# When batch 1's query, scores and soft maximum are placed in the second Y phase

## Chip, cores and metric

The kernel runs on one core of a Trainium2 chip. The metric is the device time of one execution in microseconds. Before the change three runs took 453.0, 452.93 and 451.36 us (median 452.93); one more execution was profiled, and it took 451.54 us.

## What is computed

The input x has 2 batches of 1024 rows of 1024 values. Every row is normalised, and two matrices are applied to it. The first is a weight in which blocks of 32 x 32 are switched off by a mask; the second is a dense weight plus a sum of eight low-rank experts, mixed with coefficients that depend on the mean row of the batch.

```python
xn = layernorm(x)                                  # rows of 1024
w  = weight * block_mask                           # 32 x 32 blocks
s  = xn @ w.T + bias
q      = xn.mean(axis=1) @ Wq.T                    # one query per batch
coeffs = softmax(q @ lora_keys.T / sqrt(128))      # 8 experts
h      = einsum('bsi,eir->bser', xn, lora_down)    # rank 64 each
delta  = einsum('be,bser,ero->bso', coeffs, h, lora_up)
y      = xn @ W_org.T + delta
out    = x + s * silu(y)
```

The coefficients are one row of 8 numbers for each batch, and they need all 1024 normalised rows of that batch.

## The kernel before

The kernel folds the experts into the dense weight: for each batch it forms W_org + sum of coeff * down * up once, as tiles of 128 x 512, and then multiplies x with it. A fold needs the eight coefficients, so the chain from the row sums to the coefficients stands ahead of the first fold of a batch.

All large products are in float32 split in two parts: a value's high part (a rounded copy made by ScalarE) and the low rest (a subtraction on VectorE). A product takes three matmuls for each 128 of the inner dimension: high x high, high x low, low x high (lines 450, 453, 454 for the rows of batch 0). A tile of 128 rows by 512 columns is thus 24 matmuls.

The work is a long list in program order. First come the masked weight and the tiles of s for batch 0's first 512 columns, then two phases called "y" for batch 0, with eight tiles each (tile 0 to 7). Between the tiles of a phase, jobs for later stages are put in. In the second Y phase they are given by `jobs_c(i)`, called behind tile i: `s_mul` and `s_lo` prepare the other half of the masked weight (`s1`), one of eight inner tiles at a time (line 297 loads `ws`, 299 masks it on VectorE, 302 copies the high part on ScalarE, 307 takes the low part on VectorE); `wide_load`, `wide_a` and `wide_b` load and normalise the columns of batch 1 (lines 962, 963), with the row sums `xsum` as a by-product, and form sums of them (968).

Behind the second Y phase follow the tiles of s for batch 0's second half, with 16 folds for batch 1 between them (4, 4, 3, 3 and 2 behind the first five s tiles). A fold is 12 matmuls (414 to 416) on `dhi`, `dlo` (the `down` weights, 405 and 406) and `cut` (the `up` weights scaled by the coefficients, 392 on ScalarE and 393 on VectorE, made by `scale_up`). The last part, some 220 us, is batch 1 itself, in seven products for each two-by-two block of tiles (line 1211).

The coefficients of batch 1 come in four steps, a tuple that `coeffs(1)` returns:

- `steps[0]`, the row transposes: eight small transposes on TensorE (322) spread `xsum` over all partitions into two PSUM tiles, `xrow`
- `steps[1]`, the query: two products with accumulation on VectorE (346), `xrow` by `Wq`, and a join (350) that writes `qb`
- `steps[2]`, the scores: one matmul of `qb` with the keys (357, two passes in the records), three small VectorE instructions (359, 361, 362) and a power on GpSimd (364)
- `steps[3]`, the soft maximum: a sum, a reciprocal and two scalings on VectorE (370, 372, 377)

A step can also be put inside a tile: `split_at[(0, 1, i)]` names a step that goes between the first and the last 12 matmuls of tile i.

TensorE, VectorE, ScalarE and GpSimd run their instructions in the written order. The order of SyncE's queue, which issues most of the loads (SP), is made by a scheduler from that list. The evacuation of a tile (475 on ScalarE in a Y phase, 466 and 499 for a final s tile) is kept pending and written ahead of the next tile. `scale_up` takes one staging buffer from `misc` (`up_homes`) and three from a ring of six tiles, which `ws`, `us`, the `down` tile and the `W_org` tile of a fold share.

Of the kernel before, what the change touches and what calls it, by code (L numbers as in the profile page):

```python
# [32 lines left out]
def kernel(  # L33
# [492 lines left out]
    split_at = {}  # L526
# [6 lines left out]
    def phase(kind, b, h, w, final, jobs):  # L533

        for i in range(TPB):
            flush()
            if (b, h, i) in split_at:
                ps, part = open_gemm(b, i, w)
                part(0, 4)
                split_at[(b, h, i)]()  # L540
                part(4, NKT)
            else:
                ps = gemm(b, i, w)
            if final:
                pending.append(J(final_evac, kind, b, h, i, ps))
            else:
                pending.append(J(tile_evac, kind, b, h, i, ps))
            for job in jobs(i):
                job()
# [100 lines left out]
    with tc.manual_schedule(engines={mybir.EngineType.PE, mybir.EngineType.DVE, mybir.EngineType.Activation, mybir.EngineType.Pool}):  # L650
# [344 lines left out]
        steps = coeffs(1)  # L995

        def jobs_c(i):
            if i < 2:
                yield J(store_out, 1 - i)
            if i == 5:  # L1000
                yield steps[0]
                yield steps[1]
            if i == 6:
                yield steps[3]
                yield J(scale_up, 1, 0, up_homes)
            if i < 6:
                yield J(s_mul, s1, 1, i)
                yield J(s_lo, s1, 1, i)
            if i == 5:
                for kt in (6, 7):  # L1010
                    yield J(s_mul, s1, 1, kt)
                    yield J(s_lo, s1, 1, kt)
            if i in (0, 2):
                yield J(wide_load, 2 + i // 2, 0)
                yield J(wide_load, 2 + i // 2, 1)
            if i < 5:
                yield J((wide_b, wide_a)[i % 2], 1 + (i + 1) // 2)

        up_homes = [misc[:, 0, :]]
        split_at[(0, 1, 6)] = steps[2]  # L1020
        phase("y", 0, 1, y01, False, jobs_c)


# [341 lines left out]
```

## Time and profile before

| | |
|---|---|
| the three runs | 453.0, 452.93, 451.36 us |
| profiled execution, whole | 451.54 us |
| its span, first to last instruction | 449.8 us |
| mean granted TensorE clock | 0.998 |
| data moved, mean | 90.58 MB, 201 GB/s |
| second Y phase, tiles 6 and 7, with steps 0 to 2 | 189.4 to 203.7 us of the span |
| first s tile of the second half | 203.7 to 209.1 us |
| first fold of batch 1 | from 209.1 us |

The profile lists instructions with their start from the span's beginning and their duration, by engine: PE is TensorE's matmul, DVE VectorE, ACT ScalarE, POOL GpSimd. An idle time ahead of an instruction is shown with what ended it. Matmuls overlap: one of 512 columns has a modelled length of 0.39 us, but the next starts 0.227 us after it. What counts is therefore the distance from start to start.

### The profile page before, as it was taken

To read this page: it belongs to the slowest core of one execution; us is meant where nothing else is said; L and a number is where in the kernel's file an instruction comes from. 1 tells how busy PE (TensorE), PEld (TensorE's weight loads), DVE (VectorE), ACT (ScalarE), POOL (GpSimd) and SP (SyncE) were. 2 spreads that over 40 slices of the span, in tenths; PEclk is the share of its full clock that TensorE was granted. 3 is DMA by queue.
4 is the path that set the end of the run, shared out by engine and by line. 5 is a ranking of instruction groups with operands and counts; after the bars stand their busy time and mean duration, and the time that the engine had idled before them with its cause. 6 is when DMAs were issued, how large, how long until landed. Compare 5 with 4: busy or idle time off the path is not lost.

```text
span 449.8 us, 5786 instructions
## 1 busy us (share of the span) xinstructions
PE 439.7 (98%) x2058; PEld 363.3 (81%) x2058; DVE 289.4 (64%) x478; ACT 175.6 (39%) x291; POOL 76.6 (17%) x93
## 2 busy tenths in 40 slices
PE   7999999999999999999999999999999999999996
PEld 5789888888888888778888788888888888888885
DVE  5989777766528758876456667487556294365615
ACT  3676626454631221225233134067344322441520
POOL 3784210002220402221000000110020030002000
PEclk9999999999999999999999999999999999999999
DMA  8995406687796887797979797966183146218103
GB/s 272 390 345 207 143 25 206 215 265 217 250 306 179 267 248 251 268 346 259 286 219 311 218 306 197 302 176 189 40 180 127 66 110 172 93 24 209 49 1 117
DMA packets 47741, 90.58 MB, mean 201 GB/s; under 512 B 4816, under 2 KB 15328, under 8 KB 47712
## 3 DMA queue, kind: packets, MB, share of 16 engines
q1 hardware_dynamic: 30624, 66.08, 43.1%
q0 software_dynamic: 6624, 16.26, 15.7%
q10 hardware_dynamic: 10464, 7.87, 5.4%
q8 instruction: 16, 0.26, 0.3%
q14 instruction: 13, 0.11, 0.1%
HBM read 70.26 MB, written 19.93 MB: 201 GB/s over the span
## 4 chain that ended last, share of the span: by engine, by line
PE 73%; issue 10%; DMA 8%; DVE 4%; POOL 3%; SPq 0%; ACT 0%; POOLq 0%; DVEq 0%; ACTq 0%
PE acc_ps L1211 25%; PE py L1211 10%; PE acc_ps L450 8%; PE acc_ps L454 8%; PE acc_ps L453 8%; PE psw L416 5%; PE psw L415 5%; PE psw L414 5%; DMA ramp<-in_wT_dram 2%; DMA keys_sb<-in_keysT_dram 2%; POOL xv L524 2%; DMA ramp<-in_mask_dram 2%; DMA misc<-in_up_dram 1%; DMA xv<-xt 1%; POOL stash L502 1%
## 5 line engine op out<-in xcount | busy, mean ns | idle before, releaser
L1211 PE MATMUL acc_ps<-xw,ow 128*128 128x512 f32 (+1 forms) x492 | 113.2, 386 | 0.0
L1211 PEld LDWEIGHTS acc_ps<-xw,ow 128*128 128x128 f32 x492 | 91.0, 188 | 19.5
L450 PE MATMUL acc_ps<-slot,xgrp 128*128 128x512 f32 (+1 forms) x288 | 106.6, 370 | 0.1
L454 PE MATMUL acc_ps<-slot,xgrp 128*128 128x512 f32 (+1 forms) x288 | 105.7, 367 | 0.7 <-DVE xgrp L603 0.7
L453 PE MATMUL acc_ps<-slot,xgrp 128*128 128x512 f32 (+1 forms) x288 | 105.7, 367 | 0.6 <-DVE slot L591 0.2
L453 PEld LDWEIGHTS acc_ps<-slot,xgrp 128*128 128x128 f32 x288 | 54.3, 189 | 10.8 <-DVE slot L591 2.1
L454 PEld LDWEIGHTS acc_ps<-slot,xgrp 128*128 128x128 f32 x288 | 54.2, 188 | 10.2 <-DVE xgrp L603 1.1
L450 PEld LDWEIGHTS acc_ps<-slot,xgrp 128*128 128x128 f32 x288 | 54.3, 189 | 9.1 <-DVE stash L466 0.3
L416 PE MATMUL psw<-cut,dlo 128*128 128x512 f32 x128 | 50.1, 391 | 0.3 <-DVE dlo L406 0.3
L414 PE MATMUL psw<-cut,dhi 128*128 128x512 f32 x128 | 49.9, 390 | 0.0
L415 PE MATMUL psw<-cut,dhi 128*128 128x512 f32 x128 | 49.8, 389 | 0.0
L1211 PE MATMUL py<-xw,ow 128*128 128x512 f32 x192 | 46.9, 392 | 0.0
L1211 PEld LDWEIGHTS py<-xw,ow 128*128 128x128 f32 x192 | 36.1, 188 | 7.9
L1104 DVE TENSOR_TENSOR ow<-raw,ow 128x1024 fp32r<-128x1024 f32 (+1 forms) x32 | 34.5, 1088 | 9.9 <-ACT ow L1103 9.9
L405 ACT CAST dhi<-ds 128x512 fp32r<-128x512 f32 x32 | 19.7, 616 | 40.8 <-DMA ds<-in_down_dram 25.2
L502 POOL DMA_DIRECT2D stash<-in_x_dram x16 | 14.4, 899 | 117.6 <-DVE stash L499 117.6
L421 DVE TENSOR_TENSOR wo<-wo,psw 128x512 f32<-128x512 f32 x32 | 21.9, 685 | 13.2 <-PE psw L416 13.0
L406 DVE TENSOR_TENSOR dlo<-ds,dhi 128x512 fp32r<-128x512 f32 x32 | 22.0, 687 | 12.6 <-ACT dhi L405 12.5
L1103 ACT CAST ow<-raw 128x1024 fp32r<-128x1024 f32 (+1 forms) x32 | 29.4, 941 | 1.8 <-DVE wo L421 1.6
L416 PEld LDWEIGHTS psw<-cut,dlo 128*128 128x128 f32 x128 | 24.0, 188 | 5.8 <-DVE dlo L406 0.9
L415 PEld LDWEIGHTS psw<-cut,dhi 128*128 128x128 f32 x128 | 24.1, 188 | 5.1
L414 PEld LDWEIGHTS psw<-cut,dhi 128*128 128x128 f32 x128 | 24.0, 188 | 4.9
(180 smaller groups left out, 468.9 us busy)
## 6 DMA issues: line engine op xcount, KB each, us to landing
ds<-in_down_dram SPq DMA_DIRECT2D x32, 256.0 KB, 3.7
wo<-in_worgT_dram SPq DMA_DIRECT2D x32, 256.0 KB, 3.7
raw<-in_x_dram SPq DMA_DIRECT2D x11, 512.0 KB, 4.9
stash<-in_x_dram POOLq DMA_DIRECT2D x16, 256.0 KB, 4.8
raw<-in_wu_dram SPq DMA_DIRECT2D x8, 512.0 KB, 4.9
yu<-wo ACTq DMA_DIRECT2D x16, 256.0 KB, 4.5
raw<-yu SPq DMA_DIRECT2D x8, 512.0 KB, 3.7
out_dram<-stash ACTq DMA_DIRECT2D x14, 256.0 KB, 4.1
```

The lines of the kernel that those rows point to most:

```text
L405: nc.scalar.copy(dhi, ds)
L406: nc.vector.tensor_tensor(dlo, ds, dhi.bitcast(F32), ALU.subtract)
L414: nc.tensor.matmul(ps, lhsT=dhi[:, c, :], rhs=u[c][:, 0, :], start=c == 0, stop=False)
L415: nc.tensor.matmul(ps, lhsT=dhi[:, c, :], rhs=u[c][:, 1, :], start=False, stop=False)
L416: nc.tensor.matmul(ps, lhsT=dlo[:, c, :], rhs=u[c][:, 0, :], start=False, stop=c == 3)
L421: nc.vector.tensor_tensor(ws, ws, ps, ALU.add)
L450: nc.tensor.matmul(ps, lhsT=xs[:, kt, 0, cols], rhs=w[:, kt, 0, wc], start=kt == 0, stop=False)
L453: nc.tensor.matmul(ps, lhsT=xs[:, kt, 0, cols], rhs=w[:, kt, 1, wc], start=False, stop=False)
L454: nc.tensor.matmul(ps, lhsT=xs[:, kt, 1, cols], rhs=w[:, kt, 0, wc], start=False, stop=kt == NKT - 1)
L1103: nc.scalar.copy(o[:, a:b, 0], raw[:, a:b])
L1104: nc.vector.tensor_tensor(o[:, a:b, 1], raw[:, a:b], o[:, a:b, 0].bitcast(F32), ALU.subtract)
L1211: nc.tensor.matmul(ps, lhsT=o[:, a, wl, j, :], rhs=xw[j][:, m, xl, cols], start=start and j == 0 and k == 0, stop=j == 3 and k == 2, skip_ ...
```

## The change

Three of the four steps for batch 1's coefficients are placed later in the second Y phase, and the last moves with them.

```diff
         def jobs_c(i):
             if i < 2:
                 yield J(store_out, 1 - i)
-            if i == 5:
-                yield steps[0]
+            if i == 6:
                 yield steps[1]
-            if i == 6:
+            if i == 7:
                 yield steps[3]
                 yield J(scale_up, 1, 0, up_homes)
             if i < 6:
                 yield J(s_mul, s1, 1, i)
                 yield J(s_lo, s1, 1, i)
             if i == 5:
                 for kt in (6, 7):
                     yield J(s_mul, s1, 1, kt)
                     yield J(s_lo, s1, 1, kt)
...
         up_homes = [misc[:, 0, :]]
-        split_at[(0, 1, 6)] = steps[2]
+        split_at[(0, 1, 6)] = steps[0]
+        split_at[(0, 1, 7)] = steps[2]
         phase("y", 0, 1, y01, False, jobs_c)
```

| step | before | after |
|---|---|---|
| row transposes | behind tile 5 | in the middle of tile 6 |
| query | behind tile 5, ahead of the last three weight tiles of `s1` | behind tile 6, and so behind those three weight tiles |
| scores | in the middle of tile 6 | in the middle of tile 7 |
| soft maximum, first `scale_up` | behind tile 6 | behind tile 7 |

On ScalarE the evacuation of tile 6 comes ahead of the four scalings instead of behind them. On SyncE two loads of `misc` for batch 1 come behind the third `up` load and the first fold's two loads instead of ahead of them. GpSimd's order is the same.

## The prediction

> **What bounds the kernel now.** I read the page first, then the waits of TensorE (PE), then the timelines of PE, VectorE (DVE) and the DMA issues around the place of the change, and last the granted clock. The page says who sets the end:
>
> ```profile
> PE 439.7 (98%) x2058; PEld 363.3 (81%) x2058; DVE 289.4 (64%) x478; ACT 175.6 (39%) x291; POOL 76.6 (17%) x93
> ```
>
> PE is busy 439.7 of 449.8 us; ten microseconds are all that it idles. So a change of order is worth what it adds to or takes from PE's idle time. The waits view, for PE, gives the idle time by what ended it:
>
> ```profile
> PE sp L357 <- DVE qb L350: 1.1, 1, 1.1
> PE xrow L322 <- DVE bd L963: 0.7, 1, 0.7
> ...
> PE psw L416 <- DVE dlo L406: 0.3, 1, 0.3
> ```
>
> The first two belong to the edited lines: the scores matmul waits 1.1 us for the query, and the row transposes wait 0.7 us for the last row sum. The third line is the only one that the same view lists for 203 us to the end. From there on nothing can absorb a delay of PE, so a shift goes to the end of the kernel one for one. The timeline of PE shows the two places:
>
> ```profile
> 189.41 0.93 PE L322 MATMUL xrow<-ident,xsum 128*128 128x128 f32 x7
> 191.00 0.32 PE L322 MATMUL xrow<-ident,xsum 128*128 128x128 f32 x1 [0.67 <-DVE bd L963]
> 191.08 0.48 PE L450 MATMUL acc_ps<-slot,xgrp 128*128 128x512 f32 x1
> ...
> 195.18 0.36 PE L357 MATMUL sp<-keys_sb,qb 128*128 128x8 f32 x2 [1.08 <-DVE qb L350]
> 195.39 0.48 PE L450 MATMUL acc_ps<-slot,xgrp 128*128 128x512 f32 x1
> ```
>
> And the timeline of DVE shows what feeds them, and what stands behind the query today:
>
> ```profile
> 192.80 0.69 DVE L968 TENSOR_TENSOR xt<-bd,tt 128x512 f32<-128x512 f32 x1
> 193.40 0.68 DVE L346 SCALAR_TENSOR_TENSOR junk<-xrow,misc 128x512 f32<-128x512 f32 x1
> ...
> 194.74 0.29 DVE L350 TENSOR_TENSOR qb<-qh 128x128 f32<-128x128 f32 x1
> 195.26 0.69 DVE L299 TENSOR_TENSOR ws<-ws,m_sb 128x512 f32<-128x512 f32 x1 [0.23 <-DMA ws<-in_wT_dram]
> 196.64 0.69 DVE L307 TENSOR_TENSOR slot<-ws,slot 128x512 fp32r<-128x512 f32 x1 [0.69 <-ACT slot L302]
> ...
> 200.60 0.69 DVE L307 TENSOR_TENSOR slot<-ws,slot 128x512 fp32r<-128x512 f32 x1 [0.69 <-ACT slot L302]
> 201.21 0.16 DVE L359 TENSOR_SCALAR sc<-sp 128x8 f32<-128x8 f32 x1
> ```
>
> The reader is to see that three weight tiles (L299, then L302 on ScalarE, then L307) hold DVE from 195.26 to 201.21, two microseconds each, and that the first of them starts when its data lands, not when DVE is free. The tile view of these loads has the same: issued from 190.1 on, landed 5.1 us later at the earliest.
>
> ```profile
> L297 SPq DMA_DIRECT2D ws<-in_wT_dram x3: 371/372/423, 190.1 to 191.1; - x3
> ...
> DMA to landing us min/median/max: 5.1/5.8/6.0
> ```
>
> Last, the windows view of PE at the end of the span, where PE has nothing to do after about 446.06 (the columns are the stretch, its length, PE busy, and then the clock):
>
> ```profile
> 447.00:448.00 1.00, 0.00 (x0) 1.00 0.09 29
> ...
> 448.30:448.50 0.20, 0.00 (x0) 0.68 0.14 41
> 448.50:449.80 1.30, 0.00 (x0) 0.50 0.00 0
> ```
>
> The granted clock falls to half at about 448.37 (0.68 over 0.2 us means 0.07 us at full), some 2.3 us after the last matmul. The longest idle time before that, 1.59 us near the start, brought no drop.
>
> [...] the scores of batch 1 leave PE at about 195.5, yet L359 reads them at 201.21, behind the three weight tiles. [...]
>
> **The change part by part.** Nothing is added or removed: 8 transposes, 2 query products, one join, one score matmul, the soft maximum and four scalings are the same instructions. On PE the transposes go behind 12 more matmuls (half of tile 6), the score matmul behind 24 more (half of tile 7). On DVE, the two L346 and L350 change places with the six instructions of the weight tiles. ACT gets tile 6's evacuation ahead of the four scalings instead of behind; POOL keeps its order.
>
> *Row transposes.* Tile 5's last matmul starts at 189.18; the next may start at 189.41. Half a tile is 12 x 0.227 = 2.7 us, so the transposes come at 192.1. Their last input is there at 190.95. The 0.67 us of waiting is gone. Eight transposes at the spacing of the row of seven (0.66 us for six steps, 0.11 each) end at 193.0.
>
> *Query.* DVE is free at 193.4 as before, but its next instruction is now the first L299, whose data lands at about 195.2. The load is issued behind two others on SP, which wait for DVE work before the edit (L962, done at 189.7), so the landing stays. The three tiles then run to 201.21 as now. The query takes 194.74 - 193.40 = 1.34 us to the start of L350, which is thus 202.55; today the score matmul follows 0.44 us after that start, so it starts at 203.0.
>
> *Scores.* PE: second half of tile 6 from 193.0 to 195.75, first half of tile 7 to 198.5. Then it stands until 203.0: a wait of 4.5 us on L357, instead of 1.08. Behind it on PE are the other 12 matmuls of tile 7, the whole of the first s tile and the folds, which everybody waits for.
>
> *Sum on PE.* After 203.0: 0.2 for the scores, then 36 matmuls (half of tile 7, s tile 0) at 0.227 = 8.2, so the first fold at 211.4; the page's trace has it at 209.13. That is +2.3 us. (By waits: 4.5 new, against 0.67 and about 1.3 with its restart removed, and about 0.2 less for rounded spacing.)
>
> *Soft maximum and scaling behind it.* Today L359 at 201.21 leads to L377 at 204.01, the first L392 at 204.51 and the first fold's dlo (L406) at 208.19 to 208.88: 7.7 us. Now L359 starts at about 203.5, so dlo is done by 211.2. It is needed by the fold's third matmul, 211.4 + 0.45. It just fits, and the tile-6 evacuation (0.58 us on ACT), no longer between the scalings and dhi, adds to the slack. Cost nothing; if the cover goes, up to 1 us. The up loads and the first down and worg loads wait on buffers that the weight tiles free at unchanged times; the two misc<-xv loads go behind them on SP and behind L346, about 8 us later, and are first used at 213.2. Nothing.
>
> *The clock.* A wait of 4.5 us is [...] longer than the 2.3 us that sufficed at the end. If the clock halves during the wait, matmuls after 203.0 run at half rate [...]. [...] a gain is excluded, as 1.00 is what is granted now. I take 1.5: about 3 us of matmuls at half rate.
>
> Total +2.3 + 1.5 = +3.8 us. The profiled execution took 451.54 us (span 449.8 and 1.7 around it): 455.3. Its three neighbours are 451.36, 452.93 and 453.0, so this is one of the two quick ones; on the mean of the four, 452.2, I get 456.0, and 456.7 on the median 452.93. I take 456.0.
>
> **The rivals.**
> *No clock drop.* The wait is as worked out, but the clock stays at 1.00. [...] Against: half clock after 2.3 us at the end. 452.2 + 2.3 = 454.5.
>
> *The scaling becomes late too.* The chain from L359 to the fold's operands has 0.6 us of slack by my sum; if the loads of up or down land later by more, the first fold waits as well. Another 1 to 2 us: 457.5. Against: a clock drop gives the chain more slack.
>
> *The other side: the waits go and none comes.* The removed 0.67 and 1.1 to 1.3 us stay saved, 450.3 us. This happens if L350 is done when PE comes to the scores at 198.5, that is, starts by 198.06. The weight tiles take 5.95 us and the query 1.34, so the first L299 would have to start at 190.8. Its data lands 4.4 us after that and DVE is busy with L968 until 193.4. It needs the query to be ahead of the weight tiles on DVE; the program order puts it behind.
>
> **How the numbers follow.** Forecast (wait and clock drop) 0.70, no drop 0.16, late scaling 0.08, other side 0.06. About 0.5% (2.26 us) is what a measurement of this kernel can tell from no change. The forecast is slower by more than that in nine of ten cases, with the spread of the four times; the no-drop case, at +2.3, in half; the late scaling always. Slower 0.70 x 0.9 + 0.08 + 0.08 = 0.79, rounded to 0.78. The other side saves at most 2.0 us, just under the bound; faster 0.04, and the same 0.18. The range runs from 453.4, low in the no-drop case, to 458.4[...].
>
> **What would show it.** Right: in PE's waits, L322 gone, L357 on L350 with 4 to 4.7 us; on DVE, L346 at about 201.2 behind the last L307; the clock at 0.50 for about 3 us from 202 to 206; the first L414 of batch 1 at about 212.9. Without a drop, that L414 is at 211.4. Wrong: a first L299 at 193.4 instead of 195.2 (the wait shrinks by up to 1.8 us), or PE waits after 210 us that are not there today.

## The result, and the profile after

The changed kernel took 457.81 us in the median of six runs (456.0 to 459.21), against 452.55 us for the kernel before beside it. The ratio is 1.011, with a 95% interval of 1.0071 to 1.0148. Two more series, measured later, gave 1.0094 (1.0058 to 1.0129) and 1.0094 (1.0055 to 1.0132). It is slower by about 1%.

The profiled execution took 456.0 us, the lowest of its six runs, with a span of 454.3 us. The waits of PE in the changed kernel, by what ended them (total, times, longest; waits of the start-up left out):

```profile
PE sp L357 <- DVE qb L350: 3.8, 1, 3.8
PE psw L416 <- DVE dlo L406: 1.1, 1, 1.1
```

The transposes (L322) no longer wait; the scores matmul waits 3.8 us where it had waited 1.1. The same place in PE's timeline (start, duration, instruction, and idle time ahead of it):

```profile
192.35 1.03 PE L322 MATMUL xrow<-ident,xsum 128*128 128x128 f32 x8
193.15 0.47 PE L450 MATMUL acc_ps<-slot,xgrp 128*128 128x512 f32 x1
...
198.47 0.39 PE L454 MATMUL acc_ps<-slot,xgrp 128*128 128x512 f32 x1
202.69 0.36 PE L357 MATMUL sp<-keys_sb,qb 128*128 128x8 f32 x2 [3.83 <-DVE qb L350]
...
204.20 0.63 PE L454 MATMUL acc_ps<-slot,xgrp 128*128 128x512 f32 x1
204.63 0.63 PE L450 MATMUL acc_ps<-slot,xgrp 128*128 128x512 f32 x1
...
207.55 0.39 PE L453 MATMUL acc_ps<-slot,xgrp 128*128 128x512 f32 x1
...
212.77 0.39 PE L414 MATMUL psw<-cut,dhi 128*128 128x512 f32 x1
```

Two things are to be seen: the hole from 198.7 to 202.69, and behind it matmuls of 0.63 us, 0.43 us from start to start where it had been 0.227, which is about half speed. The windows view of PE dates that (stretch, length, PE busy, clock, and then the DMA engines' share and GB/s):

```profile
202.00:204.00 2.00, 1.31 (x7) 1.00 0.98 353
204.00:206.00 2.00, 2.00 (x7) 0.51 0.92 344
206.00:208.00 2.00, 2.00 (x7) 0.63 0.15 50
208.00:210.00 2.00, 2.00 (x10) 1.00 0.43 121
```

A mean of 0.51 over 2 us is 0.04 us at full clock, and 0.63 is 0.52 us: half clock from 204.04 to 207.48, 3.4 us. DVE's timeline has the cause of the hole:

```profile
194.96 0.69 DVE L299 TENSOR_TENSOR ws<-ws,m_sb 128x512 f32<-128x512 f32 x1 [1.44 <-DMA ws<-in_wT_dram]
...
200.30 0.69 DVE L307 TENSOR_TENSOR slot<-ws,slot 128x512 fp32r<-128x512 f32 x1 [0.69 <-ACT slot L302]
200.91 0.68 DVE L346 SCALAR_TENSOR_TENSOR junk<-xrow,misc 128x512 f32<-128x512 f32 x1
...
202.25 0.29 DVE L350 TENSOR_TENSOR qb<-qh 128x128 f32<-128x128 f32 x1
```

DVE stands idle for 1.44 us with the query's input ready (the transposes end at about 193.1), because the next instruction in its order is a weight tile whose data has not landed. The query follows the third tile.

The sum closes on the spans. From the end of tile 5 to the first fold it was 209.13 - 189.41 = 19.72 us; now it is 212.77 - 189.63 = 23.14 (the transposes' start less 12 matmuls of 0.227), so +3.4. From the first fold to the end of the last matmul it was 236.9 and is 237.75, +0.8, which is a wait at a later fold (L416, at 252.65) of 1.1 where 0.3 had been. The start-up gives 0.2. Together +4.5 us, 454.3 - 449.8. The two `misc` loads that the change also moved were issued at 201.6 instead of 194.1, and their first user, at 216.85 on ScalarE, did not wait for them.

### The profile page after: what moved, and what is told of

Read it like the earlier page. It is cut to its first block, busy times and chain, and to the rows that moved or that the text cites. A ratio compares the mean times of both kernels' runs of the same rounds, so it can differ in the third digit from the quotient of the medians.

```text
span 454.3 us, 5792 instructions
## 1 busy us (share of the span) xinstructions
PE 441.7 (97%) x2058; PEld 365.2 (80%) x2058; DVE 289.7 (64%) x478; ACT 175.6 (39%) x291; POOL 76.4 (17%) x93
## 4 chain that ended last, share of the span: by engine, by line
PE 67%; DVE 11%; DMA 9%; issue 7%; ACT 4%; POOL 2%; SPq 0%; ACTq 0%; POOLq 0%; DVEq 0%
PE acc_ps L1211 24%; PE py L1211 10%; PE acc_ps L454 6%; PE acc_ps L450 6%; PE acc_ps L453 6%; PE psw L416 4%; PE psw L415 4%; PE psw L414 4%; DMA ws<-in_wT_dram 3%; DMA stash<-in_x_dram 2%; DVE st L145 1%; DMA yu<-wo 1%; DVE slot L591 1%; DMA raw<-in_mask_dram 1%; ACT slot L302 1%
## 5 line engine op out<-in xcount | busy, mean ns | idle before, releaser
L416 PE MATMUL psw<-cut,dlo 128*128 128x512 f32 x128 | 50.0, 391 | 1.1 <-DVE dlo L406 1.1
L416 PEld LDWEIGHTS psw<-cut,dlo 128*128 128x128 f32 x128 | 24.0, 188 | 6.5 <-DVE dlo L406 1.6
```

The costliest lines, as they stand in the source:

```text
L416: nc.tensor.matmul(ps, lhsT=dlo[:, c, :], rhs=u[c][:, 0, :], start=False, stop=c == 3)
```

## Experiments

Two theories were held against each other first: the cost is VectorE's order (query behind weight tiles), or it is the later place on TensorE. Then the half clock was to be priced by itself, and the landing of the weight loads. The edits are shown in part, against the changed kernel; that of "Only the scores later" is against the kernel before.

### The query ahead of the weight tiles again

```diff
             if i == 6:
                 yield steps[1]
...
-            if i < 6:
+            if i < 5:
                 yield J(s_mul, s1, 1, i)
                 yield J(s_lo, s1, 1, i)
-            if i == 5:
-                for kt in (6, 7):
+            if i == 6:
+                for kt in (5, 6, 7):
                     yield J(s_mul, s1, 1, kt)
                     yield J(s_lo, s1, 1, kt)
```

> The changed kernel, but the query is written ahead of the last three weight tiles, so VectorE has the order of the kernel before; the transposes and the scores stay where the change put them. If the order on VectorE is the cost: the scores matmul (L357) no longer waits for the query, the clock stays at full in mid-run, and what is left is a wait of 1 to 1.5 us at the first fold's dlo, since the soft maximum still starts behind the weight tiles at about 201.2; time 0 to 0.8 us under the kernel before, some 5 us under the changed kernel. If the later place on TensorE is the cost: within 1 us of the changed kernel.

Measured: 451.61 us, ratio to the kernel before 0.9977 (0.996 to 0.9993). The waits of PE have no line for L357, and the clock stays at full. What is left at the first fold is in PE's timeline:

```profile
199.37 0.28 PE L357 MATMUL sp<-keys_sb,qb 128*128 128x8 f32 x2
208.26 0.50 PE L414 MATMUL psw<-cut,dhi 128*128 128x512 f32 x1 [0.30 <-ACT dhi L405]
208.60 0.40 PE L415 MATMUL psw<-cut,dhi 128*128 128x512 f32 x1
209.29 0.51 PE L416 MATMUL psw<-cut,dlo 128*128 128x512 f32 x1 [0.30 <-DVE dlo L406]
```

The transposes and the scores are where the change put them, and the kernel is not slower. So the order on VectorE carries the loss, and neither the later places on TensorE nor ScalarE's changed order, which this kernel keeps, does. The removed waits of 1.8 us come back only in part: the first fold waits 0.6 us for its operands, less than the 1 to 1.5 us that were expected.

### Only the scores later

```diff
             if i == 5:
                 yield steps[0]
                 yield steps[1]
-            if i == 6:
+            if i == 7:
                 yield steps[3]
                 yield J(scale_up, 1, 0, up_homes)
...
-        split_at[(0, 1, 6)] = steps[2]
+        split_at[(0, 1, 7)] = steps[2]
```

> The kernel before with one part of the change: scores in the middle of tile 7, soft maximum and first scaling behind tile 7; transposes and query stay behind tile 5. If a later place of the scores on TensorE costs by itself: slower than before, as the changed kernel. If VectorE's order costs: the query is there at about 194.7, the scores matmul at 199.3 waits for nothing, the transposes wait 0.7 us as before, no half clock in mid-run, and 0 to 1 us under the kernel before.

Measured: 451.51 us, ratio 0.9973 (0.9954 to 0.9992). In the waits of PE the transposes' line stays and that of the scores is gone:

```profile
PE psw L416 <- DVE dlo L406: 0.8, 2, 0.5
...
PE xrow L322 <- DVE bd L963: 0.6, 1, 0.6
```

A later place of the scores on TensorE does not cost; with the query in its old place it gains 0.3%.

### Filling the wait: what the half clock costs

```diff
+        def filled_scores():
+            fill_ps = ps_w.tile([P, NH], F32, name="fill_ps", tag="psw")
+            for k in range(16):
+                nc.tensor.matmul(
+                    fill_ps, lhsT=xg[(0, 1)][:, k % 4, 0, :P], rhs=y01[:, k % 4, 0, :], start=True, stop=True
+                )
+            steps[2]()
+
-        split_at[(0, 1, 7)] = steps[2]
+        split_at[(0, 1, 7)] = filled_scores
```

> The changed kernel with 16 extra matmuls of 512 columns (3.6 us), whose result nobody reads, in front of the scores matmul, inside its wait. VectorE's order and the wait for the query stay. If the half clock is a cost of its own: the scores start at 202.7 as before, the clock stays at full, the first fold starts at about 211.3 instead of 212.8, and the median falls by 1.5 to 3.5 us against the changed kernel. If the half clock is a by-product that costs nothing beyond the wait: the same time as the changed kernel.

Measured: 454.44 us, ratio 1.0039 (1.0024 to 1.0055). PE's timeline, and then its waits:

```profile
199.40 3.79 PE L1023 MATMUL fill_ps<-slot,xgrp 128*128 128x512 f32 x16
204.13 0.36 PE L357 MATMUL sp<-keys_sb,qb 128*128 128x8 f32 x2 [0.95 <-DVE qb L350]
212.63 0.39 PE L414 MATMUL psw<-cut,dhi 128*128 128x512 f32 x1
```

```profile
PE psw L416 <- DVE dlo L406: 1.2, 1, 1.2
```

From the scores to the first fold it is 8.50 us here and 10.08 in the changed kernel's profile: the half clock costs 1.6 us there, for the same 36 matmuls. In this execution the first weight tile started 3.35 us behind the transposes' start, against 2.61, so the scores came 0.7 us later behind the transposes than in the changed kernel's profile. In the medians the fill saves 2.5 us against the series measured beside it (454.44 against 456.9), and up to 3.4 against the others (457.81). On the mean of all 17 runs of the changed kernel it is 2.8 (457.4 less 454.6), which is more than one 3.4 us stretch at half clock can lose, 1.7. The next two runs look for the rest.

### Half the fill

The same edit with `range(8)`, which leaves some 2.2 us of idle time. In the kernel before the clock fell some 2.3 us behind the last matmul; the question is whether 2.2 us in mid-run bring half clock too, or whether the clock stays at full.

> The changed kernel with 8 extra matmuls (1.8 us) in front of the scores matmul, so that TensorE idles some 2.2 us there instead of 4. [...] half clock in mid-run and the time of the changed kernel. [...] full clock and the time of the kernel with 16 extra matmuls, about 454.5 us[...].

Measured: 455.6 us, ratio 1.0062 (1.0045 to 1.0079), between the two. Its profile has a wait of 2.2 us and half clock again (timeline and windows of PE):

```profile
198.08 1.97 PE L1023 MATMUL fill_ps<-slot,xgrp 128*128 128x512 f32 x8
202.25 0.57 PE L357 MATMUL sp<-keys_sb,qb 128*128 128x8 f32 x2 [2.19 <-DVE qb L350]
```

```profile
202.00:204.00 2.00, 1.75 (x5) 0.53 1.00 323
204.00:206.00 2.00, 2.00 (x7) 0.62 0.35 134
```

The clock fell at 202.12 (0.53 over 2 us is 0.12 us at full), after 2.1 us of idle time, which were enough in this execution. Of the 17 runs 12 had a mean clock of 0.996 or less; the other five had 0.998 to 1.0, so the drop is not sure at this length. (The mean clock counts the half clock behind the last matmul too, but the seven profiles without half clock in mid-run have 0.998 to 1.0, so that takes off 0.002 at most. One stretch of 3.4 us takes off 0.004.)

### The changed kernel, twice more

> The changed kernel once more, for a second profile. The wait for the query and the order repeat: scores at 202.5 to 203, the wait some 3.8 us. The half clock [...] 3.4 us or 6.8 us of it in mid-run, and the time follows, 456 to 459 us. If the spread of the times comes from data movement instead, the clock is the same and PE's other waits differ.

Measured: 456.9 us. The second profile repeats the first: scores at 203.81 behind a wait of 4.0, the fold 10.08 later, half clock for 3.4 us. It has no wait at the later fold.

> The changed kernel a third time, to see in a profile what the slower half of its runs has (clock 0.991 to 0.992). [...] half clock for 6.8 us in mid-run and the first fold 1.5 us later than in the first two profiles. If this execution is of the quick half: the half clock lasts 3.4 us again, and the fold follows the scores matmul by about 10.1 us.

Measured: 457.41 us, and this profile has the longer stretch (windows of PE):

```profile
200.00:202.00 2.00, 0.36 (x2) 1.00 1.03 420
202.00:204.00 2.00, 0.00 (x0) 0.61 1.02 409
204.00:206.00 2.00, 1.62 (x5) 0.50 0.99 368
206.00:208.00 2.00, 2.00 (x7) 0.50 0.87 321
208.00:210.00 2.00, 2.00 (x8) 0.69 0.08 26
```

Half clock from 202.44 to 209.24, 6.8 us, twice as long. Two of these microseconds fall into the wait itself, so the scores are followed by the fold after 10.78 us, 0.7 more than in the other two profiles, not the 1.5 that the expectation gave for this case. Over the three series the changed kernel has 17 runs. Eight have a mean clock of 0.994 to 0.996 and take 455.2 to 457.4, mean 456.2. Nine have 0.991 or 0.992 and take 457.3 to 459.6, mean 458.4. With the filled wait (0.998 to 1.0 in 18 of 19 runs) the median is 454.4. The steps are 1.8 and 2.1 us; half of 3.4 us is 1.7. One stretch of 3.4 us and the end of the span can't bring the mean below 0.994, so the nine runs had more half clock than that; 6.8 us take off 0.007. But where the further part lies is known for the profiled run alone, and there it cost 0.7 us; this run had also reached the transposes 1.5 us later than the first profile. That it makes the whole step of 2.1 us is therefore not shown.

### The weight loads issued earlier

```diff
+            if i == 4:
+                yield J(s_load, 1, 5)
+                yield J(s_load, 1, 6)
+            if i == 5:
+                yield J(s_load, 1, 7)
```

`s_load` takes the staging tile and issues the load from ScalarE's queue; `s_mul` then uses that tile.

> The changed kernel, with the loads of the last three weight tiles issued from ScalarE's queue, two of them a tile earlier and one in the same place, so that they don't stand behind the two raw loads on SyncE's queue. If their landing is a term of the wait: the first L299 starts when VectorE is free, 1.3 to 1.6 us earlier, the wait at the scores matmul is 2.3 to 2.6 us instead of 3.8 to 4.0, and the median 1.2 to 2 us under the changed kernel; half clock still in mid-run, since 2.2 us were enough for it. If something else holds the weight tiles: no difference.

Measured: 457.01 us, ratio 1.0092 (1.0073 to 1.0111). On DVE the first tile no longer waits for its data, and PE's wait is shorter by 1.0 to 1.2 us (timeline of DVE, then waits of PE; the edit moved the line numbers, L308 is L299 and L366 is L357):

```profile
193.92 0.68 DVE L308 TENSOR_TENSOR ws<-ws,m_sb 128x512 f32<-128x512 f32 x1
```

```profile
PE sp L366 <- DVE qb L359: 2.8, 1, 2.8
...
PE psw L425 <- DVE dlo L415: 1.2, 1, 1.2
...
PE acc_ps L1225 <- ACT acc_ps L1285: 0.6, 1, 0.6
```

The landing is a term of the wait, as the profile shows. The expected gain of 1.2 to 2 us did not come: the time lies within the intervals of the changed kernel. In this profile two later waits, 1.8 us together, took the gain back. That they always do is not shown, but five of the six runs have a mean clock of 0.996 and take 456.2 to 457.3 us, no less than the runs of the changed kernel with a mean clock of 0.994 to 0.996.

### Better orders

With the query first, the three small instructions on the scores can go between the weight tiles as well. Three variants were run. In the first, the scores stand between tiles 6 and 7, and the soft maximum ahead of the last weight tile:

```diff
+            if i < 5:
+                yield J(s_mul, s1, 1, i)
+                yield J(s_lo, s1, 1, i)
             if i == 6:
                 yield steps[1]
-            if i == 7:
+                yield J(s_mul, s1, 1, 5)
+                yield J(s_lo, s1, 1, 5)
+                yield steps[2]
+                yield J(s_mul, s1, 1, 6)
+                yield J(s_lo, s1, 1, 6)
                 yield steps[3]
+                yield J(s_mul, s1, 1, 7)
+                yield J(s_lo, s1, 1, 7)
                 yield J(scale_up, 1, 0, up_homes)
...
-        split_at[(0, 1, 7)] = steps[2]
```

> Transposes in the middle of tile 6, query ahead of the weight tiles, scores between tiles 6 and 7, the soft maximum's steps between the weight tiles, the scaling behind them. If VectorE's order is what counts: neither transposes nor scores wait, the first fold starts at about 206.9 instead of 209.1 without waiting, 1.8 to 2.4 us under the kernel before. If a later wait takes the place (the fold's dlo, or the first s tile on its last weight tile): 0 to 1 us under it.

Measured: 451.77 us, ratio 0.9982 (0.9968 to 0.9996). The expected gain of 2 us did not come: the scores still wait 0.4 us, and the first fold starts at 209.00, where 206.9 was said. ACT's timeline names what was late at the first fold:

```profile
207.14 0.72 ACT L392 ACTIVATE cut<-us,c 128x512 fp32r<-128x512 f32 x1 [1.80 <-DMA us<-in_up_dram]
```

This `up` load was issued at 198.59, when the first weight tile had given its buffer back, and landed 8.5 us later. An earlier soft maximum can't help ahead of that load.

In the second variant the scores stay in the middle of tile 7 and only the last weight tile stands between them and the soft maximum:

```diff
+            if i < 5:
+                yield J(s_mul, s1, 1, i)
+                yield J(s_lo, s1, 1, i)
             if i == 6:
                 yield steps[1]
+                for kt in (5, 6):
+                    yield J(s_mul, s1, 1, kt)
+                    yield J(s_lo, s1, 1, kt)
             if i == 7:
+                yield J(s_mul, s1, 1, 7)
+                yield J(s_lo, s1, 1, 7)
                 yield steps[3]
...
```

> As the kernel with the query ahead of the weight tiles, but the three small instructions on the scores and the soft maximum stand on VectorE ahead of the last weight tile and behind it, so that GpSimd's power runs beside that tile. If the soft maximum's start behind the weight tiles is what the first fold still waits for: its dlo 1 to 1.5 us earlier, no wait on dlo there, 1.3 to 1.8 us under the kernel before. If the loads of up and down are (issued when a weight tile frees its buffer, landing 7 us later): the fold waits for dhi, and the time is that of the kernel with the query ahead, about 1 us under.

Measured: 451.16 us, ratio 0.9961 (0.9943 to 0.9979), the lowest ratio of all: 1.7 us under the kernel before beside it (452.87), as expected. But its interval overlaps with those of the other orders that are quicker than the kernel before, so which is the best is not shown. Its profile still has waits of 0.7 (dhi) and 0.3 us (dlo) at the first fold.

The third adds the early loads of the section before to the second.

> The kernel with the scores' instructions between the weight tiles, and the three early loads as well. If the first weight tile's landing is what is left there (it waited 1.3 us): the chain to the first fold's dlo is 1 to 1.3 us earlier, the first fold waits for nothing, and the median is 0.5 to 1.2 us under that kernel, 2 to 3 us under the kernel before. If the first fold's own loads (up, down) set its start: within 0.4 us of that kernel.

Measured: 451.92 us, ratio 0.9979 (0.9966 to 0.9993). That is no gain over the second variant, where 0.5 to 1.2 us were expected. In the profile the first fold comes at 207.30, the earliest of all, and the waits list nothing for it. But from there to the end of the last matmul it takes 238.65 us, against 237.89 in the second variant's profile and 236.9 in that of the kernel before. So an earlier first fold is not kept to the end. That part of the kernel is not as rigid as the prediction took it.

## Why the prediction was right

**What bounds the kernel: right in the main.** PE's busy time and the two waits were read rightly, and the whole loss is on PE. "A shift goes to the end one for one" was too strict: the first fold came 3.4 us later and the span grew by 4.5 in one profile, while the early loads brought the first fold forward by 1.0 us and the time by nothing clear, and the last variant brought it forward by 2.2 us against the kernel before (from the end of tile 5) and the time by 1.2 in the medians. The later wait on L416 is 0 to 1.2 us in different profiles. In the changed kernel's profile its chain goes back to a `misc` load that landed at 249.5 and, by way of ScalarE, held up VectorE's queue; why it differs from one execution to the next stays open.

**Row transposes: right.** Said: start at 192.1, no wait, done at 193.0. Measured: 192.35, no wait, and the next matmul at 193.15.

**Query: right.** Said: first L299 at 195.2 by its load's landing, L346 at 201.2, L350 at 202.55. Measured: 194.96, 200.91 and 202.25. The early loads removed the landing and moved the query, and the query ahead of the tiles removed the wait altogether.

**Scores: right, a little too long.** Said: 4.5 us of wait, scores at 203.0. Measured: 198.70 to 202.69 from start to start, 4.0, and 3.8 to 4.0 in the wait view of three profiles. Without the half clock the profile's first fold would come 1.8 us later than before (3.4 less 1.6), where 2.3 was said; in the medians the filled wait costs 1.7 us (454.44 against 452.77).

**Soft maximum and scaling: right.** Said: it just fits. In the changed kernel the first fold waits for nothing. The filled wait has the late query without the half clock: its `dlo` is done at about 211.95 and needed at 213.09, a slack of 1.1 us where 0.6 was said.

**The clock: the drop right, its size too small.** The term was 1.5 us, from "about 3 us of matmuls at half rate". That length was the author's estimate: the trace of the kernel before has no half clock in mid-run to read it from. One stretch of 3.4 us costs 1.6 in the profile. But nine of 17 runs had more half clock than one such stretch, and they take 2.1 us more, of which the one profile of such a run shows 0.7. By the medians, the loss over the filled wait is 2.5 to 3.4 us in the three series, against the 1.5 of the forecast. The wait was put 0.5 us too high and the clock 1 to 2 us too low, so the total of +3.8 came nearer to the measured +4.1 to 5.3 than its terms did: that part is luck.

**The rivals.** "No clock drop" is what the filled wait built: 454.5 was said and 454.44 measured. The agreement is partly luck, since the rise was 1.7 us and not 2.3, from a kernel before that took 452.77 and not 452.2. "The other side" needed the query ahead of the weight tiles; with that order the kernel took 451.61, 1.2 us under the one before, not 1.9, since the fold's operands were the next to be late. "The scaling becomes late too" did not happen at the first fold.

## What to carry to other kernels

A step that is moved later on one engine also changes its place in the queue of another; look at what it is put behind there, and at what that work waits for. Here a query of 1.6 us went behind three tiles that wait for a load, and TensorE stood still for 4 us. And count an idle stretch of TensorE like this one at more than its length: here 4 us of it brought half clock for 3.4 or 6.8 us, which by the medians cost 2.5 to 3.4 us on top of the wait. Filling the hole with matmuls that nobody reads won more than half of the loss back.

## What the runs showed of the hardware

Five of the twelve profiles have half clock in mid-run: 3.4 us of it in four, 6.8 us in the changed kernel's third. Where the clock fell differs. In the half-filled kernel that was in the idle time, 2.1 us after its start (200.05 to 202.12). In the third profile of the changed kernel it was in the idle time too, 2.1 us after the last matmul's end at 200.36, with the fall at 202.44 (timeline of PE):

```profile
199.97 0.39 PE L454 MATMUL acc_ps<-slot,xgrp 128*128 128x512 f32 x1
204.38 0.56 PE L357 MATMUL sp<-keys_sb,qb 128*128 128x8 f32 x2 [4.02 <-DVE qb L350]
```

In the first profile TensorE had been idle for 3.8 us up to 202.69, and had worked for 1.35 us again when the clock fell at 204.04. In the seven profiles without half clock in mid-run, those of the kernel before and its relatives among them, waits of up to 2.0 us brought no fall.

So 2.1 us of idle time were enough in one execution of the half-filled kernel, but its wait of some 2.2 us brought the mean clock to 0.996 or less in only 12 of 17 runs. What else decides, and what sets the length of the half clock, is not shown.

In the changed kernel the last three weight loads, of 256 KB each, landed 4.8 to 6.0 us after their issue, and the three `up` loads behind them 5.8 to 6.4; in the kernel before it was 5.1 to 6.0 and 6.5 to 8.0. The slowest that was seen, the third `up` load in the first of the better orders, took 8.5 us from 198.59. All DMA engines together moved 408 GB/s from 200 to 205 us, most of its way.
